# Setup of a gated cross-attention kernel: loads on two queues, 32x32 transposes on VectorE, and the memory projection with its chunks outermost

## Chip, cores and metric

The kernel runs on one core of a Trainium2 chip. The metric is the device time of one execution in microseconds (us), the median of several runs; lower is better. A core has TensorE (PE: matmuls; PEld: its weight loads), VectorE (DVE), ScalarE (ACT), GpSimd (POOL) and SyncE (SP), which here only issues DMAs. "SPq" and "ACTq" are the instruction streams of SyncE and ScalarE where they issue DMAs.

## What is computed

x is 8 x 1024 x 1024 and the memory 8 x 64 x 512, all float32. Reduced to what matters:

```python
mp   = einsum('bme,de->bmd', memory, W_mem)             # 8 x 64 x 1024
s    = einsum('bnd,bmd->bnm', x, mp) / sqrt(1024)
c    = einsum('bnm,bmd->bnd', softmax(s), mp)
gate = sigmoid(concat([x, c]) @ W_gate.T + b_gate)
f    = x + gate * c
out  = f * rsqrt(mean(f*f, -1) + 1e-6) * norm_w
```

The gate's product is split in two. The half of W_gate that meets c is multiplied with the 512 rows of mp once (G2 = mp @ W2 + b_gate), since softmax(s) @ G2 then gives that half for each token. The half that meets x (W1) is multiplied with x in the main loop, by a scheme with seven products in two levels that needs sums of blocks of x and of W1.

## The kernel before, in words

**Setup**, then a **main loop** over 16 tiles of 512 tokens. The change touches the setup alone. `pin` keeps each instruction behind what was written earlier for the same engine, so the order of the source is the order of each engine and of each queue. `load` (L95) issues on SyncE's queue, `scratch` (L98) on ScalarE's.

1. **Loads**, all on SyncE's queue: the memory (`mem_sb`, L117, four of 128 partitions), W_mem (`wm`, L121, four of 128 partitions), the bias, half of W2's columns (`load_w2(0)`, L138, 16 loads of 128 KB into four of the seven `gate` buffers), W1 (`ws`, L143 to L149, 32 loads of 128 KB). W2 and W1 come in quarters of 32 partitions.
2. **Memory transposed** on TensorE (`pt_mem`, L165, against an identity) into PSUM, copied by VectorE to `memT` (L171). VectorE reorders W_mem's columns into `wmp` (L179).
3. **Projection, transposed** (`pm`, L195 to L204): for each of eight blocks of 128 output features, four chunks of 128 of the contraction. ScalarE and VectorE copy the results by turns to `mpT`; each pair goes to DRAM (`mpd`).
4. **mp by rows** (`pt_mp`, L206 to L221): 32 transposes on TensorE, eight copies on ScalarE, eight DMAs to DRAM (`mgd`).
5. **G2** (`pg`, L400 to L424): eight groups (n = 0 to 7; column half h, row block q), each of eight matmuls of 128x512 in one of five PSUM banks. VectorE adds the bias into one of two stages used by turns; two DMAs on ScalarE's queue carry a stage to `mgd`. After n = 0 come the loads of W2's other half (`load_w2(1)`), of x's first tile (`xq`, L251, 16 loads) and of `nw_sb`. After each of n = 0 to 5 VectorE does a sixth of the sums of W1 (`w1_tasks`: four `outer_sum` of 128x2048, 28 inner sums of 128x512), and after n = 6 the first transposes and sums of x (`first`), with GpSimd's `inner_s` behind them.

The main loop then starts with products `kA` to `kF` (L576), which use the same five PSUM banks; its work is laid out in slots by hand (`plan`, L436). A float32 matmul shows as two records (x2) in the profile.

Tile buffers are named by tags. The four `xq` buffers hold W_mem, then mp by rows, then x.

Of the kernel before, what the change touches and what calls it, by code (L numbers as in the profile page):

```python
# [8 lines left out]
F32 = mybir.dt.float32  # L9
# [6 lines left out]
P = 128  # L16
# [4 lines left out]
def tile_gated_cross_attention_rmsnorm(  # L21
# [40 lines left out]
    nc = tc.nc  # L62
    B, N, D = x.shape
    M, E = mem.shape[1:]
# [3 lines left out]
    BM = B * M  # L68
    KD = D // P
    KE = E // P  # L70
    H = 512
    C = 256
    NPAIR = BM // P
    SCALE = 1.0 / float(D) ** 0.5
    Q4 = D // 4
# [3 lines left out]
    xqpool = ctx.enter_context(tc.tile_pool(name="xqpool", bufs=4))  # L79
    apool = ctx.enter_context(tc.tile_pool(name="apool", bufs=1))  # L80
    rot = ctx.enter_context(tc.tile_pool(name="rot", bufs=2))
    small = ctx.enter_context(tc.tile_pool(name="small", bufs=1))
    ps = ctx.enter_context(tc.tile_pool(name="ps", bufs=1, space=PSUM))
    ps_ctx = ctx.enter_context(tc.tile_pool(name="ps_ctx", bufs=2, space=PSUM))
    dram = ctx.enter_context(tc.tile_pool(name="dram", bufs=1, space=DRAM))

    pin = tc.keep_in_program_order

    def mm(o, lhsT, rhs, start, stop):
        pin(nc.tensor.matmul(o, lhsT, rhs, start=start, stop=stop, skip_group_check=True))  # L90
# [4 lines left out]
    def load(o, i):  # L95
        pin(nc.sync.dma_start(o, i))

    def scratch(o, i):  # L98
        pin(nc.scalar.dma_start(o, i))

    def t4k(pool, shape, tag, name):
        return pool.tile(shape, F32, tag=tag, name=name)
# [7 lines left out]
    def bank(n, shape, name):  # L110
        return ps.tile(shape, F32, tag=banks[n % 5], name=name)


    memr = mem.rearrange("b m e -> (b m) e").rearrange("(q p) e -> p q e", p=P)
    mem_sb = [t4k(rot, [P, 2, E], "l2", f"mem_sb{i}") for i in range(2)]
    for q in range(NPAIR):
        load(mem_sb[q // 2][:, q % 2, :], memr[:, q, :])  # L117
    wm = []
    for k in range(KE):
        t = t4k(xqpool, [P, D], "xq", f"wm{k}")  # L120
        load(t, w_mem_t[k * P : (k + 1) * P, :])  # L121
        wm.append(t)
    bias_sb = t4k(small, [P, D], "junk", "bias_sb")
    load(bias_sb, b_gate.partition_broadcast(P))
    w2r = rows_by_chunk(w_gate_t[D:, :])
    w2 = {}

    def load_w2(h):
        for k in range(KD // 2):
            t = t4k(gpool, [P, 2, H], "gate", f"w2_{k}_{h}")  # L130
            for i in range(4):
                load(
                    t[32 * i : 32 * (i + 1), :, :],
                    w2r[i][:, 2 * k : 2 * k + 2, h * H : (h + 1) * H],
                )
            w2[k, h] = t

    load_w2(0)  # L138

    w1r = rows_by_chunk(w_gate_t[:D, :])  # L140
    ws = {o: const.tile([P, 7, 2, C], F32, name=f"ws{o}") for o in range(1, 8)}
    R11, R21, R12, R22, T4, T1, T2 = range(7)
    for o, k, h in ((1, 0, 0), (7, 0, 1), (3, 1, 1), (2, 1, 0)):  # L143
        for i in range(4):
            for n in range(2):
                load(
                    ws[o][32 * i : 32 * (i + 1), 2 * n : 2 * n + 2, :, :],
                    w1r[i][:, 4 * k : 4 * k + 4, h * H + n * C : h * H + (n + 1) * C],
                )  # L149
    nw_sb = const.tile([P, D], F32, name="nw_sb")  # L150

    ident = const.tile([P, P], F32, name="ident")
# [3 lines left out]


    mpd = dram.tile([P, KD, BM], F32, name="mpd")
    mgd = dram.tile([B, 2, M, D], F32, name="mgd")
    memT = [t4k(apool, [P, 2, BM], f"a1{i + 1}", f"memT{i}") for i in range(2)]  # L160
    for q in range(NPAIR):
        pt = bank(q, [P, KE, P], f"pt_mem{q}")
        for k in range(KE):
            pin(
                nc.tensor.transpose(  # L165
                    pt[:, k, :], mem_sb[q // 2][:, q % 2, k * P : (k + 1) * P], ident
                )
            )
        for i in range(2):
            pin(  # L170
                nc.vector.tensor_copy(  # L171
                    memT[i][:, :, q * P : (q + 1) * P], pt[:, 2 * i : 2 * i + 2, :]
                )
            )
    wmp = []
    for k, tag in enumerate(("a21", "a22", "s1", "s2")):
        t = t4k(apool, [P, KD, P], tag, f"wmp{k}")
        pin(
            nc.vector.tensor_copy(  # L179
                t.rearrange("p j (i r) -> p j i r", r=32),  # L180
                wm[k].rearrange("p (i j r) -> p j i r", i=4, r=32),
            )
        )
        wmp.append(t)

    mpT = [
        t4k(rot, [P, 2, BM], tag, f"mpT_{tag}_{i}")
# [4 lines left out]
    def mp_rows(j, q):  # L192
        return mpT[j // 2][:, j % 2, q * P : (q + 1) * P]

    for j in range(KD):  # L195
        pm = bank(j, [P, BM], f"pm{j}")
        for k in range(KE):
            mm(pm, wmp[k][:, j, :], memT[k // 2][:, k % 2, :], k == 0, k == KE - 1)
        dst = mpT[j // 2][:, j % 2, :]
        if j % 2 == 0:  # L200
            pin(nc.scalar.copy(dst, pm))
        else:
            pin(nc.vector.tensor_copy(dst, pm))
            scratch(mpd[:, j - 1 : j + 1, :], mpT[j // 2])  # L204

    for q in range(NPAIR):  # L206
        stage = t4k(xqpool, [P, D], "xq", f"mp{q}")
        for h in range(2):
            pt = bank(2 * q + h, [P, 4, P], f"pt_mp{q}_{h}")
            for j in range(4):  # L210
                pin(nc.tensor.transpose(pt[:, j, :], mp_rows(4 * h + j, q), ident))
            pin(
                nc.scalar.copy(
                    stage.rearrange("p (i j r) -> p j i r", i=4, r=32)[
                        :, 4 * h : 4 * h + 4, :, :
                    ],
                    pt.rearrange("p j (i r) -> p j i r", r=32),
                )
            )
        for i in range(2):  # L220
            scratch(mgd[2 * q + i, 0], stage[i * M : (i + 1) * M, :])  # L221


    def outer_sum(o, a, b):
        tt(nc.vector, ws[o][:, 0:4, :, :], ws[a][:, 0:4, :, :], ws[b][:, 0:4, :, :], ALU.subtract)

    def inner_sums(o):
        w = ws[o]
        for s, a, b in ((T1, R12, R11), (T2, R22, T1), (R12, R22, R12), (T4, R21, T2)):
            yield lambda s=s, a=a, b=b: tt(  # L230
                nc.vector, w[:, s, :, :], w[:, a, :, :], w[:, b, :, :], ALU.subtract
            )


    w1_tasks = [
        lambda: outer_sum(5, 7, 1),
        *inner_sums(1),
        lambda: outer_sum(6, 3, 5),
        lambda: outer_sum(7, 3, 7),
        lambda: outer_sum(4, 2, 6),  # L240
    ] + [f for o in (6, 7, 5, 4, 2, 3) for f in inner_sums(o)]


    xq, A, S, L2, O = {}, {}, {}, {}, {}
# [59 lines left out]
    def inner_s(q, o, part):  # L304
        l11, l12, l21, l22 = quarters(left(q, o))
        if part == 0:
            L2[q, o] = t4k(rot, [P, 4, 2, P], "l2", f"l2_{q}_{o}")
        s1, s2, s3, s4 = (L2[q, o][:, i, :, :] for i in range(4))
        if part == 0:
            tt(nc.gpsimd, s1, l21, l22, ALU.add)  # L310
            tt(nc.gpsimd, s2, s1, l11, ALU.subtract)
        else:
            tt(nc.gpsimd, s3, l11, l21, ALU.subtract)
            tt(nc.gpsimd, s4, l12, s2, ALU.subtract)
# [71 lines left out]

    def load_mg(b):
        mgs[b] = t4k(small, [P, D], "mg", f"mg{b}")
        load(mgs[b], mgd[b].rearrange("g m d -> (g m) d"))


    first = [
# [6 lines left out]
    done, n = 0, 0  # L399
    for h in range(2):  # L400
        cols = slice(h * H, (h + 1) * H)
        for q in range(NPAIR):
            pg = bank(n, [P, H], f"pg2_{h}_{q}")
            for k in range(KD):
                mm(pg, mp_rows(k, q), w2[k // 2, h][:, k % 2, :], k == 0, k == KD - 1)
            pool, tag = ((apool, "s4"), (small, "attnT"))[n % 2]
            stage = t4k(pool, [P, H], tag, f"g2_{h}_{q}")
            tt(nc.vector, stage, pg, bias_sb[:, cols], ALU.add)
            for i in range(2):
                scratch(mgd[2 * q + i, 1][:, cols], stage[i * M : (i + 1) * M, :])  # L410
            if n == 0:
                load_w2(1)
                for t in (0, 1, 2, 3):
                    load_xq(0, t)
                load(nw_sb, norm_w.partition_broadcast(P))
            if n < 6:
                while done < len(w1_tasks) * (n + 1) // 6:
                    w1_tasks[done]()
                    done += 1
            elif n == 6:  # L420
                for f in first:
                    f()
                for part in range(2):
                    inner_s(0, 1, part)  # L424
            n += 1
    load_mp(0)
    load_mg(0)
# [326 lines left out]
```

## Time and profile before

| | us |
|---|---|
| median of three runs (1009.38, 1011.12, 1463.22) | 1011.12 |
| the profiled execution's own time | 1009.18 |
| its span, first to last instruction | 1007.4 |
| PE busy in the span | 978.7 |
| DVE, POOL, ACT busy | 760.2, 688.0, 324.7 |
| first `pm` matmul starts | 9.04 |
| first `pg` matmul starts | 44.56 |
| first `kA` matmul starts | 105.83 |

The profile is of one execution. A row of the timeline gives the start of a group of instructions, the time that it took, its engine, line, operation and tiles (out<-in), how many there are, and in brackets how long the engine was idle before it and what ended the wait. The waits view sums up, for each engine and line, what it waited for. A row of the windows view gives, for a stretch, each engine's busy time, then PEclk (the granted TensorE clock, 1.00 is full), the mean busy share of the 16 DMA engines, and what they moved in GB/s.

### The profile page before, as it was taken

Reading aid. Unit: us, or ns where it says so; the run is one execution under the profiler, and the core shown is the slowest. Engines: PE = TensorE matmul, PEld = TensorE weight load, DVE = VectorE, ACT = ScalarE, POOL = GpSimd, SP = SyncE. Lnnn points to the kernel's source line nnn. Section 1 sums busy time; section 2 is a strip of 40 time slices with the busy share of each in tenths; the row PEclk is TensorE's granted clock in tenths of the full one; section 3 lists DMA queues with packets and bytes.
Section 4 is the critical chain, followed back from the end, with each engine's and each line's share of the span. In section 5 each row is a group of like instructions: output and inputs, shape, how many; then the busy total and the mean of one; then the engine's idle time right before and its main releaser. Section 6 shows DMA issues by size and latency. Waiting matters only on the chain.

```text
span 1007.4 us, 14639 instructions
## 1 busy us (share of the span) xinstructions
PE 978.7 (97%) x4976; PEld 765.6 (76%) x4976; DVE 760.2 (75%) x1478; ACT 324.7 (32%) x600; POOL 688.0 (68%) x851
## 2 busy tenths in 40 slices
PE   7898999999999999999999999999999999999995
PEld 3443688888878887888888788878888887888883
DVE  2075667878878787878788787878787887878777
ACT  0200023334241523333342415233333424152344
POOL 0000577878878687878788786878787887868772
PEclk9999999999999999999999999999999999999998
DMA  8676508263633727182715546181826363372512
GB/s 255 198 182 180 135 1 178 84 138 97 157 101 84 188 78 164 63 185 87 163 60 130 141 104 158 52 199 63 178 83 137 96 167 97 84 188 89 142 63 84
DMA packets 76522, 126.79 MB, mean 126 GB/s; under 512 B 16288, under 2 KB 53152, under 8 KB 76448
## 3 DMA queue, kind: packets, MB, share of 16 engines
q1 hardware_dynamic: 65312, 88.11, 30.1%
q0 software_dynamic: 8640, 31.46, 17.0%
q10 hardware_dynamic: 2496, 6.29, 2.1%
q8 instruction: 39, 0.64, 0.3%
q14 instruction: 35, 0.29, 0.1%
HBM read 85.98 MB, written 39.85 MB: 125 GB/s over the span
## 4 chain that ended last, share of the span: by engine, by line
PE 79%; DVE 14%; DMA 3%; issue 2%; SPq 1%; ACT 1%; ACTq 0%; POOL 0%; DVEq 0%
PE kA L90 16%; PE pc L90 11%; PE kE L90 9%; PE kF L90 8%; PE kD L90 8%; PE kB L90 8%; PE kC L90 7%; PE psT L90 6%; DVE gate L520 4%; DVE gate L93 3%; PE pm L90 2%; PE pg L90 2%; DVE e L93 2%; DVE u L93 1%; DMA mgd<-g 1%
## 5 line engine op out<-in xcount | busy, mean ns | idle before, releaser
L93 POOL TENSOR_TENSOR gate<-gate,u 128x256 f32<-128x256 f32 x336 | 269.2, 831 | 122.3 <-DVE u L93 100.8
L93 POOL TENSOR_TENSOR l<-a 128x256 f32<-128x256 f32 x128 | 125.6, 981 | 163.3 <-DVE a L267 100.0
L491 ACT ACTIVATE gate<-gate 128x512 f32<-128x512 f32 x128 | 79.1, 629 | 397.7 <-DVE gate L93 397.6
L90 PE MATMUL kA<-ws,a 128*128 128x256 f32 x512 | 131.7, 380 | 0.4 <-ACT u L634 0.4
L90 PE MATMUL pc<-mg,attnT 64*128 64x256 f32 x512 | 127.4, 389 | 0.0
L520 DVE SCALAR_TENSOR_TENSOR gate<-gate,ss,nw_sb 128x512 f32<-128x512 f32 x120 | 116.5, 980 | 1.1
L90 PE MATMUL kC<-ws,l 128*128 128x256 f32 x448 | 115.1, 379 | 0.8 <-DVE g L93 0.8
L90 PE MATMUL kD<-ws,l 128*128 128x256 f32 x448 | 115.0, 379 | 0.0
L90 PE MATMUL kB<-ws,l 128*128 128x256 f32 x448 | 115.0, 379 | 0.0
L90 PE MATMUL kF<-ws,l 128*128 128x256 f32 x448 | 115.0, 379 | 0.0
L90 PEld LDWEIGHTS pc<-mg,attnT 64*128 64x128 f32 x512 | 90.6, 186 | 29.7 <-issue 21.2
L90 PEld LDWEIGHTS kA<-ws,a 128*128 128x128 f32 x512 | 97.0, 190 | 14.7 <-ACT u L634 1.2
L90 PE MATMUL kA<-ws,s 128*128 128x256 f32 x384 | 100.3, 384 | 1.1 <-ACT u L634 1.1
L90 PEld LDWEIGHTS kB<-ws,l 128*128 128x128 f32 x448 | 85.1, 190 | 11.6
L90 PEld LDWEIGHTS kF<-ws,l 128*128 128x128 f32 x448 | 85.1, 190 | 11.6
L90 PEld LDWEIGHTS kC<-ws,l 128*128 128x128 f32 x448 | 83.8, 190 | 11.8 <-POOL l L93 1.1
L90 PEld LDWEIGHTS kD<-ws,l 128*128 128x128 f32 x448 | 83.9, 190 | 10.7
L93 DVE TENSOR_TENSOR gate<-gate,pc 128x512 f32<-128x512 f32 x128 | 87.1, 680 | 5.5 <-ACT gate L491 5.5
L267 DVE STREAM_TRANSPOSE a<-xq 128x512 f32<-128x512 f32 x128 | 86.0, 693 | 0.0
L90 PEld LDWEIGHTS kA<-ws,s 128*128 128x128 f32 x384 | 71.6, 190 | 16.7 <-DVE a L93 6.2
L93 POOL TENSOR_TENSOR l<-s 128x256 f32<-128x256 f32 x96 | 77.9, 811 | 8.0 <-PE kF L90 5.4
L93 DVE TENSOR_TENSOR u<-u,kB 128x256 f32<-128x256 f32 x112 | 46.8, 418 | 46.2 <-PE kB L90 40.2
(94 smaller groups left out, 1695.4 us busy)
## 6 DMA issues: line engine op xcount, KB each, us to landing
xq<-in_x SPq DMA_DIRECT2D x256, 128.0 KB, 5.5
gate<-in_x POOLq DMA_DIRECT2D x60, 512.0 KB, 7.5
out<-gate SPq DMA_DIRECT2D x60, 512.0 KB, 2.6
w<-in_w_gate_t SPq DMA_DIRECT2D x32, 128.0 KB, 3.4
ws<-in_w_gate_t SPq DMA_DIRECT2D x32, 128.0 KB, 3.1
mg<-mgd SPq DMA_DIRECT2D x8, 512.0 KB, 3.6
wm<-in_w_mem_t SPq DMA_DIRECT2D x4, 512.0 KB, 6.4
mgd<-mp ACTq DMA_DIRECT2D x8, 256.0 KB, 4.4
```

The source lines that it names most:

```text
L90: pin(nc.tensor.matmul(o, lhsT, rhs, start=start, stop=stop, skip_group_check=True))
L93: pin(eng.tensor_tensor(o, a, b, op))
L267: nc.vector.transpose(A[key][:, :, r * P : (r + 1) * P].rearrange("p j (s c) -> p s j c", c=32), xq[q, t].rearrange("p s (j r) -> p s j r" ...
L491: pin(nc.scalar.activation(g, g, AF.Sigmoid))
L520: nc.vector.scalar_tensor_tensor(g[:, cols], g[:, cols], rstd[:, t % 2 : t % 2 + 1], nw_sb[:, cols], ALU.mult, ALU.mult,)
```

## The change

The loads of the setup are divided between the two queues. The memory is loaded with its 128-column quarters on the four partition quarters (eight loads, runs of 512 bytes), and W_mem in quarters of 32 partitions (16 loads). All of W2 is asked for at the start, and W1 comes on ScalarE's queue. VectorE transposes the memory in 32x32 blocks straight into `memT`, and later `mpT` into `mpq`; TensorE's transposes and ScalarE's copies in the setup are gone. The projection runs over its four chunks outermost, with the eight results in eight PSUM banks (the first chunk in two halves of the columns); VectorE alone copies them out. `mgd` is laid out so that a stage of G2 leaves in one DMA, and mp by rows in 16 DMAs. W1's sums are spread over n = 0 to 4; x's first transposes come after n = 5, its sums after n = 6.

```diff
-    def scratch(o, i):
+    def load2(o, i):
         pin(nc.scalar.dma_start(o, i))
...
-    for q in range(NPAIR):
-        load(mem_sb[q // 2][:, q % 2, :], memr[:, q, :])
+    memq = [t4k(rot, [P, BM // 64, E // 4], "l2", f"memq{i}") for i in range(2)]
+    memr = mem.rearrange("b m e -> (b m) e").rearrange(
+        "(g s c) (i e) -> g i c s e", g=2, c=32, i=4
+    )
+    wm = [t4k(xqpool, [P, D], "xq", f"wm{k}") for k in range(KE)]
+    wmr = w_mem_t.rearrange("(i j r) d -> i j r d", i=4, r=32)
+    queues = (load, load2)
+    for g in range(2):
+        for i in range(4):
+            queues[g](memq[g][32 * i : 32 * (i + 1), :, :], memr[g, i])
     for k in range(KE):
-        load(t, w_mem_t[k * P : (k + 1) * P, :])
+        for i in range(4):
+            queues[k % 2](wm[k][32 * i : 32 * (i + 1), :], wmr[i, k])
-    load(bias_sb, b_gate.partition_broadcast(P))
+    load2(bias_sb, b_gate.partition_broadcast(P))
...
-    load_w2(0)
+    for h in range(2):
+        load_w2(h)
...
-                load(
+                load2(
                     ws[o][32 * i : 32 * (i + 1), 2 * n : 2 * n + 2, :, :],
...
+    def transpose_mem(g, i):
+            nc.vector.transpose(
+                memT[i][:, :, g * (BM // 2) : (g + 1) * (BM // 2)].rearrange(
+                    "p j (s c) -> p s j c", c=32
+                ),
+                memq[g].rearrange("p s (j r) -> p s j r", r=32)[:, :, 2 * i : 2 * i + 2, :],
+            )
...
+    transpose_mem(0, 0)
+    order_wm(0)
+    transpose_mem(1, 0)
+    order_wm(1)
+    transpose_mem(0, 1)
+    transpose_mem(1, 1)
+    order_wm(2)
+    order_wm(3)
...
+    mpq = [t4k(xqpool, [P, 4, Q4], "xq", f"mpq{g}") for g in range(4)]
+    pm = [bank(j, [P, BM], f"pm{j}") for j in range(5)]
+    pm += [ps_ctx.tile([P, BM], F32, tag="ctx", name=f"pm{j}") for j in (5, 6)]
+    pm += [ps.tile([P, BM], F32, tag="sc", name="pm7")]
+    for k in range(KE):
+        for cols in ([slice(0, BM // 2), slice(BM // 2, BM)] if k == 0 else [slice(0, BM)]):
+            for j in range(KD):
+                mm(pm[j][:, cols], wmp[k][:, j, :], memT[k // 2][:, k % 2, cols],
+                    k == 0 and cols.start == 0, k == KE - 1)
     for j in range(KD):
+        pin(nc.vector.tensor_copy(mpT[j // 2][:, j % 2, :], pm[j]))
+    for j in range(0, KD, 2):
+        src = mpT[j // 2]
+        load2(mpd[:, j : j + 2, :], src)
+        for g in range(4):
+                nc.vector.transpose(
+                    mpq[g].rearrange("p s (j r) -> p s j r", r=32)[:, :, j : j + 2, :],
+                    src[:, :, g * P : (g + 1) * P].rearrange("p j (s c) -> p s j c", c=32),
+                )
+    for g in range(4):
+        for i in range(4):
+            load2(mgd[0, g * P : (g + 1) * P, i * Q4 : (i + 1) * Q4].rearrange(
+                    "(s c) e -> c s e", c=32), mpq[g][32 * i : 32 * (i + 1), :, :])
...
-            for i in range(2):
-                scratch(mgd[2 * q + i, 1][:, cols], stage[i * M : (i + 1) * M, :])
+            load2(mgd[1, q * P : (q + 1) * P, cols], stage)
             if n == 0:
-                load_w2(1)
...
-            if n < 6:
-                while done < len(w1_tasks) * (n + 1) // 6:
+            if n < 5:
+                while done < len(w1_tasks) * (n + 1) // 5:
...
-            elif n == 6:
-                for f in first:
+            elif n == 5:
+                for f in first[:6]:
                     f()
                 for part in range(2):
                     inner_s(0, 1, part)
+            elif n == 6:
+                for f in first[6:]:
+                    f()
```

More of the change, by code (lines that the diff above doesn't have):

```diff
@@ L111, in bank @@
         return ps.tile(shape, F32, tag=banks[n % 5], name=name)
-    memr = mem.rearrange("b m e -> (b m) e").rearrange("(q p) e -> p q e", p=P)
-    mem_sb = [t4k(rot, [P, 2, E], "l2", f"mem_sb{i}") for i in range(2)]
-    for q in range(NPAIR):
-        load(mem_sb[q // 2][:, q % 2, :], memr[:, q, :])
-    wm = []
+    memq = [t4k(rot, [P, BM // 64, E // 4], "l2", f"memq{i}") for i in range(2)]
[8 more added lines that the diff above has]
+            queues[g](memq[g][32 * i : 32 * (i + 1), :, :], memr[g, i])
     for k in range(KE):
-        t = t4k(xqpool, [P, D], "xq", f"wm{k}")
-        load(t, w_mem_t[k * P : (k + 1) * P, :])
-        wm.append(t)
+        for i in range(4):
+            queues[k % 2](wm[k][32 * i : 32 * (i + 1), :], wmr[i, k])
     bias_sb = t4k(small, [P, D], "junk", "bias_sb")
-    load(bias_sb, b_gate.partition_broadcast(P))
+    load2(bias_sb, b_gate.partition_broadcast(P))
     w2r = rows_by_chunk(w_gate_t[D:, :])
@@ L142, in tile_gated_cross_attention_rmsnorm, with load_w1 @@
     R11, R21, R12, R22, T4, T1, T2 = range(7)
-    for o, k, h in ((1, 0, 0), (7, 0, 1), (3, 1, 1), (2, 1, 0)):
+    def load_w1(o, k, h):
         for i in range(4):
             for n in range(2):
-                load(
+                load2(
                     ws[o][32 * i : 32 * (i + 1), 2 * n : 2 * n + 2, :, :],
@@ L149, in tile_gated_cross_attention_rmsnorm @@
                 )
+    for o, k, h in ((1, 0, 0), (7, 0, 1), (3, 1, 1), (2, 1, 0)):
+        load_w1(o, k, h)
     nw_sb = const.tile([P, D], F32, name="nw_sb")
@@ L158, in tile_gated_cross_attention_rmsnorm, with order_wm @@
     mpd = dram.tile([P, KD, BM], F32, name="mpd")
-    mgd = dram.tile([B, 2, M, D], F32, name="mgd")
+    mgd = dram.tile([2, BM, D], F32, name="mgd")
     memT = [t4k(apool, [P, 2, BM], f"a1{i + 1}", f"memT{i}") for i in range(2)]
[L161 to L167, printed above, removed]
-            )
-        for i in range(2):
[L170 to L174, printed above, removed]
+    def transpose_mem(g, i):
+        pin(
+            nc.vector.transpose(
[3 more added lines that the diff above has]
+                memq[g].rearrange("p s (j r) -> p s j r", r=32)[:, :, 2 * i : 2 * i + 2, :],
+            )
+        )
     wmp = []
-    for k, tag in enumerate(("a21", "a22", "s1", "s2")):
-        t = t4k(apool, [P, KD, P], tag, f"wmp{k}")
+    def order_wm(k):
+        t = t4k(apool, [P, KD, P], ("a21", "a22", "s1", "s2")[k], f"wmp{k}")
         pin(
@@ L193, in mp_rows @@
         return mpT[j // 2][:, j % 2, q * P : (q + 1) * P]
-    for j in range(KD):
[L196 to L211, printed above, removed]
-            pin(
[L213 to L217, printed above, removed]
-                )
-            )
-        for i in range(2):
-            scratch(mgd[2 * q + i, 0], stage[i * M : (i + 1) * M, :])
+    mpq = [t4k(xqpool, [P, 4, Q4], "xq", f"mpq{g}") for g in range(4)]
@@ new lines, in tile_gated_cross_attention_rmsnorm @@
+    pm = [bank(j, [P, BM], f"pm{j}") for j in range(5)]
[4 more added lines that the diff above has]
+            for j in range(KD):
+                mm(
+                    pm[j][:, cols],
+                    wmp[k][:, j, :],
+                    memT[k // 2][:, k % 2, cols],
+                    k == 0 and cols.start == 0,
+                    k == KE - 1,
+                )
@@ new lines, in tile_gated_cross_attention_rmsnorm @@
+    for j in range(KD):
+        pin(nc.vector.tensor_copy(mpT[j // 2][:, j % 2, :], pm[j]))
[3 more added lines that the diff above has]
+        for g in range(4):
+            pin(
+                nc.vector.transpose(
+                    mpq[g].rearrange("p s (j r) -> p s j r", r=32)[:, :, j : j + 2, :],
+                    src[:, :, g * P : (g + 1) * P].rearrange("p j (s c) -> p s j c", c=32),
+                )
+            )
+    for g in range(4):
+        for i in range(4):
+            load2(
+                mgd[0, g * P : (g + 1) * P, i * Q4 : (i + 1) * Q4].rearrange(
+                    "(s c) e -> c s e", c=32
+                ),
+                mpq[g][32 * i : 32 * (i + 1), :, :],
+            )
@@ L239, in tile_gated_cross_attention_rmsnorm @@
         lambda: outer_sum(7, 3, 7),
+        *(f for o in (7, 5) for f in inner_sums(o)),
         lambda: outer_sum(4, 2, 6),
-    ] + [f for o in (6, 7, 5, 4, 2, 3) for f in inner_sums(o)]
+        *(f for o in (6, 4, 2, 3) for f in inner_sums(o)),
+    ]
     xq, A, S, L2, O = {}, {}, {}, {}, {}
@@ L388, in load_mg @@
         mgs[b] = t4k(small, [P, D], "mg", f"mg{b}")
-        load(mgs[b], mgd[b].rearrange("g m d -> (g m) d"))
+        for g in range(2):
+            load(mgs[b][g * M : (g + 1) * M, :], mgd[g, b * M : (b + 1) * M, :])
     first = [
@@ L408, in tile_gated_cross_attention_rmsnorm @@
             tt(nc.vector, stage, pg, bias_sb[:, cols], ALU.add)
-            for i in range(2):
-                scratch(mgd[2 * q + i, 1][:, cols], stage[i * M : (i + 1) * M, :])
+            load2(mgd[1, q * P : (q + 1) * P, cols], stage)
             if n == 0:
-                load_w2(1)
                 for t in (0, 1, 2, 3):
```

## Prediction

> **What bounds the kernel now.** I read the page's busy shares first, then PE's timeline of the setup, then SP's waits, then windows for the DMA rate. The page:
>
> ```profile
> PE 978.7 (97%) x4976; PEld 765.6 (76%) x4976; DVE 760.2 (75%) x1478; ACT 324.7 (32%) x600; POOL 688.0 (68%) x851
> ...
> PE   7898999999999999999999999999999999999995
> ...
> PEclk9999999999999999999999999999999999999998
> ```
>
> PE is busy nearly throughout, so only holes in PE can be won. They lie in the setup, before `kA` at 105.83; the main loop after it takes 1007.4 - 105.83 = 901.6 us and isn't edited. PE's timeline (start, time taken):
>
> ```profile
> 9.04 1.97 PE L90 MATMUL pm<-memT,wmp 128*128 128x512 f32 x4 [1.56 <-DVE wmp L179]
> ...
> 12.44 25.16 PE L90 MATMUL pm<-memT,wmp 128*128 128x512 f32 x58 [0.15 <-DVE wmp L179]
> 37.44 0.60 PE L211 MATMUL pt_mp<-ident,mpT_l 128*128 128x128 f32 x4
> ...
> 44.56 5.40 PE L90 MATMUL pg<-w,mpT_l 128*128 128x512 f32 x8 [2.14 <-ACT mp L213]
> 49.79 3.60 PE L90 MATMUL pg<-w,mpT_u 128*128 128x512 f32 x8
> 53.22 3.60 PE L90 MATMUL pg<-w,mpT_l 128*128 128x512 f32 x8
> ...
> 73.82 3.60 PE L90 MATMUL pg<-w,mpT_l 128*128 128x512 f32 x8
> 79.11 1.98 PE L90 MATMUL pg<-w,mpT_u 128*128 128x512 f32 x4 [1.69 <-DMA w<-in_w_gate_t]
> 83.44 1.96 PE L90 MATMUL pg<-w,mpT_u 128*128 128x512 f32 x4 [2.34 <-DMA w<-in_w_gate_t]
> 85.23 3.60 PE L90 MATMUL pg<-w,mpT_l 128*128 128x512 f32 x8
> ...
> 105.83 1.03 PE L90 MATMUL kA<-ws,a 128*128 128x256 f32 x4
> 106.69 1.03 PE L90 MATMUL kB<-ws,l 128*128 128x256 f32 x4
> 108.47 1.10 PE L90 MATMUL kC<-ws,l 128*128 128x256 f32 x4 [0.75 <-DVE g L93]
> ```
>
> Undisturbed, eight records start 53.22 - 49.79 = 3.43 us apart, 0.429 each. From 9.04 to 105.83 PE runs 64 `pm` and 128 `pg` records, 82.4 us of the 96.8; the other 14.4 are the holes: (a) waits for `wmp`: 12.44 - 9.04 - 6 x 0.429 = 0.8; (b) the `pt_mp` stretch with ScalarE's copies: 44.56 - (12.44 + 58 x 0.429) = 7.2; (c) the slow eight after it: 49.79 - 44.56 - 3.43 = 1.8; (d) W2's second half late: 85.23 - 73.82 - 6.86 = 4.6. Then (e) 0.75 before `kC`, whose bank waits for the last `g`.
>
> Why (d)? SP's waits (engine, what for: total us, times, longest):
>
> ```profile
> SPq L96 <- DMA mgd<-g: 26.4, 8, 5.0
> SPq L96 <- DMA mpd<-mpT_u: 9.6, 1, 9.6
> SPq L96 <- DMA mpd<-mpT_l: 8.1, 2, 4.5
> ```
>
> SP only loads inputs here, yet it waits for ScalarE's stores. In the trace all these DMAs share eight completion semaphores in turn, and an issue waits until the last DMA with its semaphore has landed. So W1's loads, ahead of W2's second half, were held back by PE's own progress. Last, the DMA rate (the two columns at the end: busy share, GB/s):
>
> ```profile
> 6.00:10.00 4.00, 2.44 (x11) 1.59 (x11) 3.19 (x8) 0.00 (x0) 0.00 (x0) 1.00 1.02 408
> 14.00:17.60 3.60, 3.60 (x9) 1.55 (x9) 0.56 (x1) 0.19 (x1) 0.00 (x0) 1.00 0.99 227
> ...
> 45.00:50.00 5.00, 5.00 (x9) 1.99 (x8) 0.00 (x0) 1.07 (x2) 0.00 (x0) 0.69 0.95 301
> ```
>
> W_mem's 128-partition loads move 408 GB/s; W2's quarters of 32 partitions 227, with the engines just as busy.
>
> [...] Nothing here has two load queues, but at a share of 0.99 there is nothing for a second one to add. [...] clock 0.69 in 45 to 50, and hole (c). [...] the trace's own price for 128x512 is 669 ns at L267, started 0.59 apart.
>
> **The change, part by part.**
>
> *Start of `pm`.* It needs `wm0` ordered. memory (1.05 MB), `wm0` and `wm1` (1.05 MB together, one on each queue, sharing the engines) come ahead of that. First data flow at about 2.6 (the first `mem_sb` load, 256 KB, landed at 3.6). All are now quarters of 32 partitions, so 2.1 MB at 227 GB/s = 9.2 us: landed at 11.8. Ordering takes 0.69 (L179) and 0.1 to pass on: PE starts at 12.6, 3.6 later than now. VectorE's first memory transpose (0.67) comes before. Bounds: 8.6 if quarters on two queues reach 408 GB/s, 13.5 if runs of 512 bytes are slower. I take 227: both queues go through the same partition quarters at the same time.
>
> Issuing isn't the limit: twelve issues on each queue, 0.47 apart as SP's are now, end at 6.4; the ninth waits for the first to land, at about 4, behind data that still flow.
>
> *Cold array.* Today `pt_mem` uses the array from 3.75, so `pm` starts warm. Now `pm` itself warms it: 1.8, the price of hole (c) (bounds 0 and 3.4).
>
> *`pm` without holes.* 27.5. The first chunk in halves costs the same columns. Chunks 2 and 3 are needed 13.7 us after the start, at 28; `wm2` and `wm3` land at 2.6 + 3.15 MB / 227 = 16.5. Hidden; uncovered, each us costs one. PE ends `pm` at 12.6 + 1.8 + 27.5 = 41.9.
>
> *`pm` to `pg`.* `pt_mem` and `pt_mp` leave PE. VectorE copies eight results at 0.69 each, behind PE's 0.86 each, the last at 42.8; `pg` needs only bank b0, free since six us, and `mpT`'s last part at its eighth matmul. So (b) and (c) vanish.
>
> *W2 and W1.* Ahead of `pg`: 3.67 MB (memory, W_mem, bias), then W2's first half and as much of W1: 4.2 MB. At 227 GB/s they are in at 37.3; `pg` starts at 41.9. Three of the second half's four tiles and all of W1 follow by 53.5, where n = 4 wants them at 41.9 + 27.5 = 69.4. The fourth waits for a `gate` buffer, freed in n = 3 at about 64, and lands by 69; wanted at 74.5. (d) vanishes. Queued behind it on SP are `xq`'s 16 loads; they also need the `xq` buffers, as below.
>
> *Stores on ScalarE's queue.* They stand behind W1's 32 loads, whose last issue is at about 50. `mpd` (2.1 MB at 408, 5 us) and `mgd`'s 16 (2.1 MB at 227, 9 us) follow: landed at about 68, which frees `xq`'s buffers. `xq` (2.1 MB, 9 us) lands at about 79; VectorE wants it after n = 5, at 83 or later. The stage of n = 0 leaves behind these, landed at about 69, so n = 2's bias addition waits from 62.7 to 69. With five banks PE doesn't notice: bank b2 is wanted again at n = 7, at 90.
>
> *Behind `xq` on SP* stand `nw_sb`, `mpb` and `mg`, the last now two issues for a batch (0.36 each). They are issued at 69 to 81, or as soon as their stores have landed; `mpb` is wanted with the first scores, some 6 us after `kA` starts (113.1 now), `mg` later still. Nothing, unless the stores are 30 us late.
>
> *VectorE.* 16 transposes of `mpT` of 128x256: between 0.33 (half of 0.67) and 0.59; I take 0.38, 6.1 in all, 42.8 to 48.9, just as n = 0 ends. Then W1's sums, 4 x 2.29 + 28 x 0.63 = 26.8, with five additions of 0.69 and the wait until 69: done at about 86. Six transposes of x (3.7), n = 6, two sums and two transposes (3.0 + 1.3): about 95, when `pg` ends at 96.8. Hidden, by under two us. So n = 7's addition finds VectorE free and (e) goes too. GpSimd's four `inner_s` (0.73 each) are done by 94.
>
> *ScalarE.* Its table load (1.28, now at 4.3) may fall ahead of its first copy; that copy is wanted 3.4 us after `kA` starts, and the last store (0.5), table load and copy (0.37) end about 3.1 after. Nothing.
>
> Sum: holes 14.4 go; later start 3.6 and cold array 1.8 come: `kA` starts at 105.8 - 9.0 = 96.8; with (e) 9.8 us. Against the profiled execution: span 997.6, own time 999.4 (1009.18 - 9.8). The median shown, 1011.12, is 1.9 above that execution: 1001.3.
>
> **Rivals.**
> 1. *VectorE becomes the bound.* VectorE's slack is under two us. With transposes at 0.59 (3.3 us) or stores landing 5 us later, n = 7's addition is 2 to 7 late, and `kC` with it: 1003 to 1009, say 1005. For it: `g`'s stage waits; against: the estimates lean to slow DMA.
> 2. *Slower than before: W1 stuck behind W2's last tile.* The four loads of that tile wait for n = 3 of `pg`. If W1's loads on ScalarE's queue have semaphores after those four in the round, none past the first few is issued before 64. Half of W1 (2.1 MB beside `xq`) then lands at 76, VectorE's remaining chain (26.8 + 3.5 + 3.7 + 0.7 + 4.3 = 39 us) ends at 116, `kC` starts there instead of at 108.5: 1011 + 8 = 1019. It decides from the point where `ws1` and `ws7` land after 69. For it: shared semaphores cost SP 44 us today. Against: the round follows the order in which issues are expected, not the source's (SP's W1 loads stand behind `mpd` stores that come later in the source).
> 3. *More gain:* loads at 408 GB/s, PE starts at 8.6 and pays 1 for the cold array: 14.4 + 0.75 + 0.4 - 1.0 = 14.6 us, 996.5.
>
> **How the numbers follow.** Likeliest 63% (own range 997 to 1003, from a start at 8.6 to 13.5); rival 1 20%; rival 2 8%; rival 3 6%; 3% for a stall that I don't see. Range 994 to 1009: it leaves out rival 2, the unseen and tails. Two per cent, about what a measurement of this kernel can tell from no change, is 20 us. The holes hold 15.2, so faster by over 2% has 0.03; slower needs rival 2 doubled or the unseen: 0.06; within: 0.91.
>
> **What would show it.** First `pm` near 12.6 with a half clock for 3.4 us; no PE idle between `pm` and `pg`, nor for `w`; `kA` near 96.8; `kC` with no wait for `g`. Wrong, if PE waits for `w` or `wmp`, if `kC` waits for VectorE, or if W1's sums start after 69.

## The result, and the profile after

| | before | after | predicted |
|---|---|---|---|
| median, us (6 runs each, side by side) | 1013.18 | 1013.5 | 1001.3 |
| the profiled execution's own time | 1009.18 | 1013.42 | 999.4 |
| its span | 1007.4 | 1011.7 | 997.6 |
| first `pm`, first `pg` | 9.04, 44.56 | 12.99, 42.54 | 12.6, 41.9 |
| first `kA`, first `kC` | 105.83, 108.47 | 102.11, 109.96 | 96.8, 98.5 |
| first `psT` (the first scores) | 113.03 | 117.39 | |

The ratio of after to before is 1.0012, 95% interval 0.9992 to 1.0033: no change that can be measured. The expected 10 us didn't come. (Of before's six executions one, at 1463.22, was disturbed and counts in the median but not in the ratio; the other five lie between 1009.38 and 1014.77, so that the profiled one is among its quickest, and the 4.3 us between the two spans are more than the ratio shows.)

The page of after, the same three lines as shown of before:

```profile
PE 975.2 (96%) x4944; PEld 766.3 (76%) x4944; DVE 766.4 (76%) x1494; ACT 317.8 (31%) x588; POOL 687.2 (68%) x851
...
PE   4998899999999999999999999999999999999995
...
PEclk9999799999999999999999999999999999999998
```

The busy totals hardly differ. What differs is where the array is slow: the fifth slice (101 to 126 us) has a clock of 0.7, which before did not have. PE's timeline says what stands there (start, time taken, engine, line, operation, tiles, count, idle before and what ended it):

```profile
12.99 29.71 PE L90 MATMUL pm<-memT,wmp 128*128 128x256 f32 x80 [12.99 <-DVE wmp L188]
42.54 3.60 PE L90 MATMUL pg<-w,mpT_l 128*128 128x512 f32 x8
...
94.04 3.60 PE L90 MATMUL pg<-w,mpT_u 128*128 128x512 f32 x8
102.11 1.94 PE L90 MATMUL kA<-ws,a 128*128 128x256 f32 x4 [4.47 <-DVE a L296]
105.74 2.04 PE L90 MATMUL kB<-ws,l 128*128 128x256 f32 x4 [1.69 <-POOL l L93]
109.96 2.05 PE L90 MATMUL kC<-ws,l 128*128 128x256 f32 x4 [2.18 <-DVE g L93]
```

Up to the last `pg` all goes as predicted: one unbroken `pm` group, then sixteen groups of `pg` 3.43 us apart, ending at 97.47. There the old 14.4 us of holes really are gone. Then PE waits three times, for x's transposes (`a`), their sums (`l`) and the last bias addition (`g`), and every group takes 1.9 to 2.05 us where before it took 1.03: the half clock (0.50 in the window 105 to 110 below). All three releasers are VectorE's work, or hang on it. VectorE's timeline shows when it fell behind:

```profile
60.06 3.22 DVE L93 TENSOR_TENSOR ws<-ws 128x512 f32<-128x512 f32 x5
84.94 0.69 DVE L93 TENSOR_TENSOR g<-pg,bias_sb 128x512 f32<-128x512 f32 x1 [21.66 <-DMA mgd<-g]
```

VectorE stands still for 21.66 us at n = 2, until a stage has left for DRAM. Its remaining chain is as long as predicted, and all of it comes that much later. ScalarE's queue shows why the store was late:

```profile
14.87 33.52 ACTq L100 DMA_DIRECT2D ws<-in_w_gate_t  x32
48.86 1.01 ACTq L100 DMA_DIRECT2D mpd<-mpT_l  x2
67.50 1.03 ACTq L100 DMA_DIRECT2D mpd<-mpT_u  x2
68.63 11.80 ACTq L100 DMA_DIRECT2D mgd<-mpq  x16
80.98 29.19 ACTq L100 DMA_DIRECT2D mgd<-g  x8
```

The first two stores of `mpd` are issued by 49.87; the third not until 67.50, though VectorE had copied its data by 42. And in the windows view the DMA engines, which predicted traffic would have filled, stand idle (the last two columns: busy share, GB/s; the one before them is the clock):

```profile
5.00:10.00 5.00, 0.00 (x0) 0.00 (x0) 0.71 (x1) 0.00 (x0) 0.00 (x0) 1.00 1.15 222
...
60.00:65.00 5.00, 5.00 (x13) 2.23 (x12) 3.21 (x6) 0.00 (x0) 0.00 (x0) 1.00 0.00 0
105.00:110.00 5.00, 2.09 (x5) 1.24 (x5) 4.78 (x7) 0.00 (x0) 2.45 (x4) 0.50 0.84 236
```

What ends at 67.5? SP's waits hold one entry of the same length:

```profile
SPq L96 <- PE pg L90: 20.0, 1, 20.0
```

SP waits 20.0 us for PE to finish n = 3, to load W2's last tile into the buffer that this frees; it issues the four loads at 65.05, and the first lands at 67.42. The trace gives the completion semaphore of each DMA: those four hold numbers 103, 105, 107 and 101 of the eight that both queues share, and `mpd`'s third store has number 103. So the store, which has nothing to do with W2, could not be issued before a load landed that itself waited for PE.

### The profile page after: what moved, and what is told of

It is laid out like the page before. It is cut to its first block, busy times and chain, and to the rows that moved or that the text cites. A ratio compares the mean times of both kernels' runs of the same rounds, so it can differ in the third digit from the quotient of the medians.

```text
span 1011.7 us, 14607 instructions
## 1 busy us (share of the span) xinstructions
PE 975.2 (96%) x4944; PEld 766.3 (76%) x4944; DVE 766.4 (76%) x1494; ACT 317.8 (31%) x588; POOL 687.2 (68%) x851
## 4 chain that ended last, share of the span: by engine, by line
PE 80%; DVE 14%; DMA 3%; issue 2%; ACTq 0%; ACT 0%; POOL 0%; DVEq 0%; SPq 0%
PE kA L90 16%; PE pc L90 11%; PE kE L90 9%; PE kD L90 8%; PE kF L90 8%; PE kB L90 8%; PE kC L90 7%; PE psT L90 6%; DVE gate L551 4%; PE pm L90 3%; DVE gate L93 3%; PE pg L90 2%; DVE e L93 2%; DVE u L93 1%; DVE ws L93 1%
## 5 line engine op out<-in xcount | busy, mean ns | idle before, releaser
L90 PEld LDWEIGHTS kC<-ws,l 128*128 128x128 f32 x448 | 84.3, 191 | 13.7 <-POOL l L93 2.9
```

## Experiments

**Theory**: the late stores come from a shared semaphore. A load that waits for its buffer holds a semaphore, the store whose turn it is next stops behind it, everything behind that on ScalarE's queue is late, and VectorE, held at the stage, becomes the bound. **Rivals**: the stores are late for another reason (too much traffic ahead of them, or the wait for the buffer itself); or VectorE is the bound whatever the stores do. All edits are to the kernel after, unless another is named; each was timed beside the kernel before on the same chip.

**free_tile** gives W2's last tile a buffer of its own, so its loads wait for nobody:

```diff
-            t = t4k(gpool, [P, 2, H], "gate", f"w2_{k}_{h}")
+            last = (k, h) == (3, 1)
+            t = t4k(small if last else gpool, [P, 2, H], "mg" if last else "gate", f"w2_{k}_{h}")
```

> W2's last tile gets a buffer that is free from the start, so that its four loads never wait for n = 3 of pg. Theory (the third mpd store waits for the semaphore of those held loads, and every store behind it on ScalarE's queue with it): the third mpd store is issued when the other two are, at about 50, mgd's stores land by about 65, VectorE waits for a stage by some 3 us at most, kA starts at 97 to 98 and kC within 3 us of it: 10 to 13 us less than the changed kernel, ratio to the kernel before about 0.989. Rival (VectorE's own work after pg starts is too long, whatever the stores do): kA stays near 102 and kC near 110, ratio about 1.00.

Measured: 1000.72 us, ratio 0.9893 [0.9868, 0.9918], span 999.0. ScalarE's queue, VectorE and PE (one fence for each):

```profile
53.56 0.97 ACTq L100 DMA_DIRECT2D mpd<-mpT_l  x2
54.88 1.61 ACTq L100 DMA_DIRECT2D mpd<-mpT_u  x2
```

```profile
74.35 0.69 DVE L93 TENSOR_TENSOR g<-pg,bias_sb 128x512 f32<-128x512 f32 x1 [10.02 <-DMA mgd<-g]
```

```profile
98.51 1.03 PE L90 MATMUL kA<-ws,a 128*128 128x256 f32 x4
...
100.24 1.03 PE L90 MATMUL kC<-ws,l 128*128 128x256 f32 x4
```

The third store now follows the second directly, the wait for the stage falls from 21.66 to 10.02 (3 at most was expected), and `kA` and `kC` wait for nothing, at full clock. With one buffer more the kernel comes near what the prediction said: a span of 999.0 where it had 997.6, `kA` at 98.51 where it had 96.8.

**late_tile** writes the same loads, and x's, later in the source, after n = 2's addition, in the hope of another hand-out of semaphores:

```diff
-    def load_w2(h):
-        for k in range(KD // 2):
+    def load_w2(h, ks=range(KD // 2)):
+        for k in ks:
...
-    for h in range(2):
-        load_w2(h)
+    load_w2(0)
+    load_w2(1, (0, 1, 2))
...
-            if n == 0:
+            if n == 2:
+                load_w2(1, (3,))
```

> The buffers stay as in the changed kernel, and W2's last tile still waits for n = 3; but its loads, and x's behind them, are written after the bias addition of n = 2, behind the mpd and mgd stores. Theory: the stores' semaphores then don't come from the held loads, and the gain is that of the free buffer to within 2 us (kA at 97 to 99, ratio about 0.989 to 0.991). If it is the wait for the buffer itself, and not the order in which semaphores were handed out, that costs: no gain, ratio about 1.00.

Measured: 1014.22 us, ratio 1.0023 [1.0012, 1.0034], span 1011.1. ScalarE's queue:

```profile
68.47 1.13 ACTq L100 DMA_DIRECT2D mpd<-mpT_u  x2
```

A miss, and one that tells nothing between the theories: the held loads again have 103, 105, 107 and 101, the third store again 103. The place in the source did not change the round.

**pool_tile** keeps the wait for the buffer, but issues the four loads on GpSimd's queue, where they get semaphores of their own (110 to 113 in the trace):

```diff
-                load(
+                put = loadp if (k, h) == (3, 1) else load
+                put(
```

> The changed kernel, with the four loads of W2's last tile issued on GpSimd's queue, whose DMAs have semaphores of their own. The tile still waits for its buffer until n = 3, and the loads still come at 65. Theory (the held loads keep a semaphore that a store then needs): mpd's third store follows the second at about 50 to 55, and the whole gain of the free buffer comes, ratio to the kernel before about 0.989. Rival (it is the wait for the buffer as such that costs): the times of the changed kernel, ratio about 1.00.

Measured: 1001.38 us, ratio 0.9885 [0.9864, 0.9907], span 999.7. The loads still come late, at 66.87, but ScalarE's queue runs on:

```profile
52.41 1.84 ACTq L103 DMA_DIRECT2D mpd<-mpT_u  x2
```

This separates the two: the wait for the buffer is there as in the changed kernel and costs nothing; the shared semaphore was what cost. It leaves open whether x's loads matter, which stand behind the held loads on SP's queue in the changed kernel and no longer do here; four_stages answers that.

**four_stages** leaves the stores late and gives VectorE four stages by turns instead of two:

```diff
-            pool, tag = ((apool, "s4"), (small, "attnT"))[n % 2]
+            pool, tag = ((apool, "s4"), (small, "attnT"), (small, "mpb"), (small, "stage"))[n % 4]
```

> The held loads and the late stores stay as in the changed kernel, but G2 has four stages instead of two, so that n = 2 and n = 3 wait for no store. Theory (the late stores cost only through the stages, by keeping VectorE idle for 21.7 us): VectorE waits at n = 4 instead, for the store of n = 0 that lands at about 85, with 25 of W1's 32 sums done; kC starts at about 100, 8 to 10 us less than the changed kernel, ratio about 0.991. If x's late loads or the late stores bind in another way, kC stays near 110.

Measured: 1001.03 us, ratio 0.9896 [0.9868, 0.9923], span 998.9. The third store is still issued at 67.50 and the stages' stores from 81.21 on. VectorE:

```profile
85.10 0.69 DVE L93 TENSOR_TENSOR g<-pg,bias_sb 128x512 f32<-128x512 f32 x1 [10.50 <-DMA mgd<-g]
```

This addition is that of n = 4, not of n = 2: the wait comes two groups later and is half as long, `kA` starts at 97.44 without a wait, and `kC` at 99.73, after a wait of 0.40. x's loads are issued from 73.90 on, as late as in the changed kernel (73.86), so their lateness isn't what costs. The late stores cost time through VectorE's stand at the stage, and the second half of the theory's chain holds too.

**before_pool** asks the same of the kernel before: its stores, on ScalarE's queue, go to GpSimd's, nothing else is changed:

```diff
     def scratch(o, i):
-        pin(nc.scalar.dma_start(o, i))
+        pin(nc.gpsimd.dma_start(o, i))
```

> The kernel before the change, with the stores of the setup (mpd, mgd) issued on GpSimd's queue, whose semaphores SyncE's loads don't share. Theory (hole d, 4.6 us, is there because SyncE's loads wait for semaphores that the stores hold): SyncE no longer waits for mpd or mgd, PE no longer waits for w at 79 and 83, kA starts at about 101, ratio about 0.995. Rival (the loads themselves are too slow): PE still waits for w, kA near 106, ratio 1.00 or above, since GpSimd's issues may be slower.

Measured: 1000.91 us, ratio 0.9882 [0.9861, 0.9904], span 999.5, `kA` at 97.90. PE's timeline:

```profile
10.00 29.11 PE L90 MATMUL pm<-memT,wmp 128*128 128x512 f32 x64 [1.54 <-DVE wmp L179]
...
42.86 3.70 PE L90 MATMUL pg<-w,mpT_l 128*128 128x512 f32 x8
```

ScalarE in before, then in before_pool:

```profile
43.43 1.07 ACT L213 COPY mp<-pt_mp 128x512 f32<-128x512 f32 x2 [1.24 <-issue]
44.53 1.55 ACTq L99 DMA_DIRECT2D mgd<-mp  x2
46.13 1.07 ACT L213 COPY mp<-pt_mp 128x512 f32<-128x512 f32 x2 [1.62 <-issue]
```

```profile
39.59 4.20 ACT L213 COPY mp<-pt_mp 128x512 f32<-128x512 f32 x8 [3.29 <-PE pt_mp L211]
```

One line wins in the old kernel what the whole change wins once its own stall is mended (free_tile). The sum against before: `pm` to the first `pt_mp` ends 1.5 later (38.95 against 37.44); the `pt_mp` stretch takes 42.86 - 38.95 = 3.9 instead of 7.1 (ScalarE's eight copies run in 4.20 us, where before its DMA issues stood between them); the slow eight after it go (1.7); W2's second half is no longer late (4.6). 3.2 + 1.7 + 4.6 - 1.5 = 8.0, and `kA` moved by 105.83 - 97.90 = 7.9. The expectation had hole (d) alone, and `kA` at 101: the move freed ScalarE as well, which it hadn't counted. GpSimd's issues were slower, as the expectation allowed (0.53 to 0.73 us for a store of `mpd`, where ScalarE had taken 0.33 to 0.35). The medians lie 12.3 us apart (1013.23 and 1000.91), since the profiled execution of before took 1009.18; the seven timed here took up to 1014.47, at granted clocks of 0.990 to 0.996, where before_pool has 0.995 to 0.997. What before loses in addition in such executions is in no profile, so the sum accounts for some 8 us of the gain and not for the rest, and the other ratios to before hold the same share that no profile shows.

**halves** (free_tile, and more) has the loads of the two queues go to different halves of the partitions, to see whether filling one half at a time holds the rate down: of the memory and W_mem, quarters 0 and 1 on SP's queue, 2 and 3 on ScalarE's; W1 begins with its upper quarters:

```diff
-        for i in range(4):
-            queues[k % 2](wm[k][32 * i : 32 * (i + 1), :], wmr[i, k])
+        for i in (0, 2, 1, 3):
+            queues[i // 2](wm[k][32 * i : 32 * (i + 1), :], wmr[i, k])
...
-        for i in range(4):
+        for i in (2, 3, 0, 1):
```

> As the kernel with the free buffer, and the setup's quarters are divided by partition: 0 to 63 on SyncE's queue and 64 to 127 on ScalarE's, for the memory and W_mem; W1's quarters run in the order 2, 3, 0, 1 while W2's run 0 to 3. Theory[...]: in 5 to 10 us the rate rises from 222 to 350 or more, the first pm matmul starts at 8 to 9 instead of 13.0, and 4 us come off the kernel with the free buffer. Rival (the small runs or the engines themselves set the rate): the rate stays under 260, and the start comes to 10 to 11 only because wm0 no longer shares the engines with wm1: 2 us.

Measured: 996.72 us, ratio 0.9855 [0.983, 0.988], span 995.0. The same window of free_tile, then of halves:

```profile
5.00:10.00 5.00, 0.00 (x0) 0.00 (x0) 0.71 (x1) 0.00 (x0) 0.00 (x0) 1.00 1.15 206
```

```profile
5.00:10.00 5.00, 0.63 (x2) 0.54 (x3) 2.02 (x3) 0.00 (x0) 0.00 (x0) 1.00 1.04 318
```

206 became 318 GB/s, between the theory's 350 and the rival's 260, with a busy share of the DMA engines above 1 in both (1.15, then 1.04), and `pm` starts at 9.37 instead of 13.31, `kA` at 93.81 instead of 98.51. warm_long and combined, below, have the same loads and move 276 and 278 in this window, so 318 is the best of three. Part of the earlier start may be that the first tile of W_mem is now loaded ahead of the second, not beside it: VectorE orders the two from 8.62 and 10.57, with a wait of 0.64 for the second's load; in the kernel after from 12.24 and 13.48, with none. W1 and W2, between 20 and 25 us, still move 239 GB/s (232 in free_tile). There the edit doesn't keep the halves apart: W2 changes its half after two loads and W1 after four, so the two queues are in the same half about half of the time, as they were without it. Whether that is the reason was not tried.

**j_outer** (halves, with the four chunks innermost again, still in eight banks) prices the order of the projection's loops:

```diff
-    for k in range(KE):
-        for cols in ([slice(0, BM // 2), slice(BM // 2, BM)] if k == 0 else [slice(0, BM)]):
-            for j in range(KD):
...
+    for j in range(KD):
+        for k in range(KE):
+            mm(pm[j], wmp[k][:, j, :], memT[k // 2][:, k % 2, :], k == 0, k == KE - 1)
```

> The kernel with its quarters divided between the queues, with the projection's chunks innermost again, as before the change, still in eight banks. Theory (the chunks outermost let PE start on wm0 alone): PE can't go on past chunk 1 until wm2 and wm3 are ordered, at about 14.5, so pg starts 4 to 5 us later, at 43 to 44 instead of 39.0, and the time is 4 to 5 us above the 996.7. If the waits for W_mem don't matter, it stays at 997.

Measured: 998.4 us, ratio 0.9858 [0.9833, 0.9883]. `pm` starts at 10.53 and waits once more, `pg` starts at 40.87 instead of 38.88: 2.0 us at that place, and the two kernels' medians differ by 1.7 (from separate comparisons, and the intervals overlap). That is less than half of what was expected. It is a price with these loads, and part of it may be that they came slower in this profile (SP's issues of W_mem end at 10.77, in halves at 10.35); with the slower loads of the change itself the order wasn't priced.

**warm** (halves with 24 TensorE transposes of the identity ahead of the projection; they are no part of the result) tries to have the array's clock full by then:

```diff
+    wt = ps.tile([P, 4, P], F32, tag="sc", name="warm")
+    for i in range(24):
+        pin(nc.tensor.transpose(wt[:, i % 4, :], ident, ident))
```

> The kernel with its quarters divided between the queues, and 24 transposes of the identity on TensorE, of no use to the result, before the first pm matmul. Theory (pm pays 1.8 us because the array is cold): pm's 80 records take about 27.8 us instead of 29.67, 1.5 to 2 us off, ratio to the kernel before about 0.984. Rival (the first chunks' waits for VectorE or for weights stretch pm): no change, 0.9855.

Measured: 997.86 us, ratio 0.9851 [0.9829, 0.9872]: no gain over halves. PE:

```profile
1.36 4.94 PE L220 MATMUL warm<-ident 128*128 128x128 f32 x24 [1.36 <-POOL ident masks.py:199]
9.97 30.71 PE L90 MATMUL pm<-memT,wmp 128*128 128x256 f32 x80 [3.67 <-DVE wmp L189]
```

After the warm-up the array stood idle for 3.67 us, and the clock was at half from 9.13 to 15.96 (0.64 in 8 to 12 us, 0.51 in 12 to 16). `pm` took 30.71 us against 29.67 in halves. The warm-up ended too early.

**warm_long** (warm, lengthened) has 52 of them (again work that is no part of the result):

```diff
-    for i in range(24):
+    for i in range(52):
```

> As warm, with 52 transposes of the identity ahead of the projection instead of 24 (they add work that is no part of the result). 24 ran from 1.36 to 6.30; at the rate of the last ones, some 0.115 us each, 28 more end near 9.5, when the first W_mem tile is ordered, so the array has no time to fall back. Theory (the warm-up of 24 failed only because the array stood idle for 3.67 us after it): no half clock in the projection, pm takes near 27.8 us instead of 29.67, pg starts near 37.5 instead of 38.88, the span near 993.5 and the ratio to before near 0.983. Rival (the half clock at the start of the projection has another cause than idleness): pm takes 29.5 or more and the ratio stays at 0.985.

Measured: 996.91 us, ratio 0.9853 [0.9826, 0.9879]. PE:

```profile
1.37 8.56 PE L220 MATMUL warm<-ident 128*128 128x128 f32 x52 [1.37 <-POOL ident masks.py:199]
10.45 27.77 PE L90 MATMUL pm<-memT,wmp 128*128 128x256 f32 x80 [0.52 <-DVE wmp L189]
...
97.53 1.10 PE L90 MATMUL kC<-ws,l 128*128 128x256 f32 x4 [2.64 <-POOL l L93]
```

On the cold array the theory is right: with 0.52 us of idleness ahead of it `pm` takes 27.77 us, as predicted for an undisturbed one (27.5), 1.9 less than in halves. The time is not shorter. `pm` started 1.1 later (in 5 to 10 us the loads moved 276 GB/s, against 318 in halves; why was not tried), and VectorE, held for 13.73 us by the stage at n = 2, finished later, so `kC` waited 2.64. (This profiled execution, 998.49, is the longest of its five.) What one stage gives, the next takes: VectorE was again the bound.

**combined** is warm_long with the edit of four_stages:

```diff
-            pool, tag = ((apool, "s4"), (small, "attnT"))[n % 2]
+            pool, tag = ((apool, "s4"), (small, "attnT"), (small, "mpb"), (small, "stage"))[n % 4]
```

> warm_long with the stages of G2 in four buffers by turns instead of two (it keeps the 52 transposes that are no part of the result). In warm_long the projection lost its half clock (27.77 us), but VectorE, held at its third bias addition by the stage, was 1.8 us later than in halves, and kC waited 2.64. Theory (with the stores as late as they are VectorE is the bound, and the warm-up can only pay once the stage no longer holds it): no addition waits more than 3 us, kA near 93.0, kC near 94.9 with no wait, so 2.6 less than warm_long: span near 994.0, ratio near 0.983. Rival (the rest is not the stage but where x's tile lands or GpSimd's sums): kC still waits over 1 us and the ratio stays at 0.985.

Measured: 995.03 us (993.96 to 995.54), ratio 0.9838 [0.9812, 0.9863], span 993.8: the fastest of all, though its interval overlaps that of halves. PE:

```profile
95.02 1.03 PE L90 MATMUL kC<-ws,l 128*128 128x256 f32 x4
```

No wait before `kC`, 13.5 us earlier than in before. One addition still waits, 4.27 us at n = 4 (at most 3 was expected), and it is made up: the last two wait for PE (2.59 and 2.08), so VectorE has slack again. Four stages without the warm-up were not tried on halves, so how much of the 1.7 us below halves each of the two gives stays open.

## Why the prediction was wrong

1. **Start of `pm`: right.** Predicted 12.6, measured 12.99; the rate was 222 GB/s where 227 was taken.
2. **Cold array and `pm`: right.** Predicted 1.8 + 27.5 = 29.3; from 12.99 to 42.54 it is 29.55. The first nine records, of 256 columns, start 0.41 to 0.58 us apart, the next of 256 columns, from 16.97 on, 0.22. warm_long shows that this comes of the lack of work ahead (27.77 with the warm-up, 29.67 in halves without). The 1.8 is not a constant: in the four kernels above that start alike (free_tile, late_tile, pool_tile, four_stages) `pm` takes from 29.20 (four_stages) to 30.79 (pool_tile).
3. **The holes (a) to (d): gone, as predicted.** `pg` runs from 42.54 to 97.47 with no wait; VectorE's 16 transposes of `mpT` came to 0.33 each (half of the 128x512 row, the low end). Only the origin of (b) was misread: before_pool has the same transposes on TensorE in 3.9 us. The other 3.2 were ScalarE's own DMA issues between its copies.
4. **"Stores on ScalarE's queue": this step failed.** The prediction counted what stood ahead of the stores on their own queue and the bytes, and had the stores land at 68, n = 0's stage at 69, and n = 2's addition wait 6.3 us. It didn't ask which semaphore each store would be given, although its own reading of before (hole (d)) was just this mechanism. The third store of `mpd` stood from 49.87 to 67.50 for semaphore 103; the stage of n = 0 landed at 84.85, some 16 late, and the addition waited 21.66. free_tile and pool_tile show that this was the cause. Even without the stall the step was optimistic: in free_tile the addition waits until 74.35, not 69, and that still costs nothing.
5. **VectorE: sizes right, slack used up.** Its chain was predicted to end at about 95 with under 2 us to spare. With 15.4 more of waiting (21.7 instead of 6.3) the work ahead of the last addition was done at 109.2, and `kC` started at 109.96 instead of 98.5.
6. **Not foreseen: the half clock.** PE's waits around `kA` cost more than themselves. From `kC` to `psT` before takes 113.03 - 108.47 = 4.6 us, after 117.39 - 109.96 = 7.4. With `kC` 1.5 later than before, 1.5 + 2.9 = 4.4, which is the difference of the spans (4.3).

So it was rival 2's mechanism with another victim, then rival 1's end. Rival 2 looked only for W1's loads behind W2's last tile; these were in time. The stores behind them, on the same queue, were not. Rival 1 allowed 5 us of lateness, not 16. The second issuing engine did not raise the rate of the change's loads (222 GB/s from two queues in 5 to 10 us, 227 from one in before, 14 to 17.6 us), and one engine's loads stopped the other's stores for 17.6 us (from 49.87 to 67.50).

Taken together, the change removed from PE the transposes (3.9 us) and the stalls, and paid with a later start and a cold array (12.99 - 9.04 = 3.95, and some 1.8). With the stall at the stage aside it comes out level: PE is through with `pg` at 97.47, in before_pool at 97.90. Keeping stores and waiting loads off each other's semaphores gets about the same in either kernel, 1.1 to 1.2% (0.9882 [0.9861, 0.9904] from before; 0.9885 [0.9864, 0.9907] with pool_tile).

## What to carry to other kernels

Here loads and stores from two queues shared eight completion semaphores, and an issue waited for the last DMA with its semaphore, whatever tensor that moved (17.6 us, from 49.87 to 67.50). Where that is so, ask for every DMA that waits for a buffer which later DMAs come round to its semaphore, on the other queue too. A load that must wait on compute belongs in a buffer of its own or on a queue with other semaphores, as in free_tile and pool_tile (1000.72 and 1001.38 us, against 1013.5). The staging buffer with two turns passed the late stores on to its engine (21.66 us of waiting at n = 2); with four, `kC` started 10.2 us earlier. Before an engine's work is moved to make room, test whether its hole is work or a stalled issue: here one word in the old kernel gained as much as the rebuilt setup did once its own stall was mended.

## What the runs showed of the hardware

- **The half clock lasted longer than the idleness ahead of it.** After 4.47 us without work, the array of the kernel after ran at half clock from 102.28 to 115.93, 13.7 us, with two more waits in it (1.69 and 2.18). In warm, 3.67 us of idleness undid the warm-up, for 6.8 us (9.13 to 15.96). In before, 2.14 us, with 0.86 shortly ahead of them, were followed by 3.41 at half clock (44.67 to 48.08). These stretches are four, two and one times 3.41 us long, and in each the last piece of 3.41 us is the first without a wait: with waits between the groups the way back took four such pieces, in before, with none, a single one. Three stretches show this, one profile each; no run varied the waits alone.
- **Loads to both halves of the partitions at once were faster.** With 32-partition quarters, three kernels that keep the two queues in different halves moved 318, 276 and 278 GB/s in 5 to 10 us (halves, warm_long, combined), the five that don't 200 to 222 (one profile each). The busy share of the DMA engines did not show this room: it was 1.15 at 206 GB/s and 1.04 at 318. The prediction had read 0.99 as nothing left for a second queue to add. In halves two queues, each on its own half, moved 318 where one queue in before had moved 227 with quarters of 32 partitions. Why the halves matter was not shown.
